# A bidirectional scan kernel: the forward direction's y is summed in PSUM instead of added afterwards

## The chip, the cores and the metric

The kernel runs on one core of a Trainium2 chip. The metric is the device time of one launch in microseconds (us). A core has TensorE (PE in the profile, its weight loads PEld), VectorE (DVE), ScalarE (ACT), GpSimd (POOL) and SyncE (SP, which issues the DMAs here). PSUM is the memory that TensorE writes into; DVE and ACT take results out of it.

## The reference, cut to what matters

The program is one convolution-attention hybrid: a selective state-space block with four scan directions, then attention without softmax, then a quantized feed-forward layer. The part that fills most of the time is the scan, for 8 images of 64 x 64 positions (L = 4096), 192 inner channels d, 16 states n and K = 4 directions:

```python
def step(h, inps):
    d_t, u_t, b_t, c_t = inps
    h = h * jnp.exp(d_t[..., None] * A) + (d_t * u_t)[..., None] * b_t[:, :, None, :]
    y = jnp.einsum('bkdn,bkn->bkd', h, c_t)
    return (h, y)
...
x_hwwh = jnp.stack([x_hw, x_wh], axis=1)
xs = jnp.concatenate([x_hwwh, jnp.flip(x_hwwh, axis=-1)], axis=1)
...
inv_y = jnp.flip(out_y[:, 2:4], axis=-1)
...
y = out_y[:, 0] + inv_y[:, 0] + wh_y + invwh_y
```

Directions 0 and 1 run forward over two orders of the positions (by rows, by columns); directions 2 and 3 run over the same two orders backwards. So y of direction 0 and of direction 2 are added position by position, and those of 1 and 3.

## The kernel before, in words

Every compute instruction is issued through a small class, `InOrder`, at one line, L91: so all rows of the profile name L91, and are told apart by their tiles. The order on each engine is fixed in advance: units of work are Python generators that `yield` an engine, a planned cost in us, a planned delay and sometimes a buffer to take, and a planner, `weave`, lets the unit go next whose engine and buffer are free first by those planned costs (rank decides ties). Each engine then runs its list strictly in that order on the chip. A changed cost or engine in one unit thus can change the order of the others.

The program has three passes. `pass1` makes the projections and the convolution, `pass2` the scans, `pass3` the rest. The change is in `pass2`. It works through 192 pieces, in order: 4 pairs of images, 3 chunks c of channels (chunks 0 and 1: the first 128 channels of one image each; chunk 2: the last 64 channels of both), 4 directions k, and 4 pieces of T = 1024 positions. For k of 2 and 3 the four pieces come in falling order of positions. An index `at` counts the pieces.

For each piece and each state n (16 of them):

- ACT makes `da` = exp(delta times A), 128 x 1024 (`decay`).
- The scan's other input is put into a `wide` tile in PSUM (two banks; there are three such tiles) in one of three ways, chosen by n: ACT scales the transposed `duT` to `x` and TensorE transposes it back into `wide` (8 transposes); POOL does the scaling (`xg`); or TensorE spreads b over the partitions (`wide<-xb,sel`) and DVE multiplies by `du` in place (`wide<-du,wide`). In chunks 0 and 1 these are 8, 2 and 6 of the 16 states, in chunk 2 they are 6, 3 and 7.
- DVE scans: `h<-da,carry,wide`. The scan ends the use of that `wide` tile. ACT keeps the last value for the next piece (`carry`).
- POOL multiplies two states at once by C, which a DMA has spread (`times_c`, the rows `c<-c,h`).
- TensorE adds these terms over n in `acc`, another PSUM tile of two banks, of which there is one: 8 transposes for each state, accumulated (`sum_over_n`, the rows `acc<-ident,c`). In pieces with k = 0 a term D times u (`ud`, made by ACT) comes first, as 8 more such transposes.

At the end of a piece `take_acc` empties `acc` into the tile `ys[k % 2]` (`y` in the profile) in SBUF: for k below 2 ACT copies it there; for k of 2 and 3 DVE adds it to what the piece of direction k - 2 at the same positions has left there. Then `acc` is free for the next piece's first sum, which waits for it. After the last piece of k = 2 and of k = 3, `store_y` writes the tile to memory, from where `pass3` reads it.

Of the kernel before, what the change touches and what calls it, by code (L numbers as in the profile page):

```python
# [42 lines left out]
P = 128  # L43
NB, HH, WW, C = 8, 64, 64, 96
L = HH * WW
DI, N, R, K = 192, 16, 6, 4
# [6 lines left out]
NT = T // P  # L53
# [5 lines left out]
GRP = 512  # L59
# [8 lines left out]
def chunk_rows(pair, c):  # L68

    b0 = 2 * pair  # L70
    if c < 2:
        return [(slice(0, P), b0 + c, slice(0, P))]
    return [(slice(64 * j, 64 * j + 64), b0 + j, slice(P, DI)) for j in range(2)]
# [456 lines left out]
def pass2(ctx, tc, g, ident, engines, fixed, u_d, xd_d, b_d, dt_d, y_d):  # L530
# [3 lines left out]
    pe, dve, act, pool = engines  # L534
# [4 lines left out]
    slots = {name: Slots(count) for name, count in room.items()}  # L539
# [4 lines left out]
    pieces = [  # L544
        (pair, c, k, NPC - 1 - i if k >= 2 else i) for pair in range(NB // 2) for c in range(3) for k in range(K) for i in range(NPC)
    ]
    done, counts, made, ys, carry = {}, {}, {}, {}, {}

    def take(name, shape, dtype=F32):

        return pools[name].tile(shape, dtype, name=name), slots[name].taken
# [203 lines left out]

    def sum_over_n(at, m):

        _, c, k, _ = pieces[at]

        def add(term, first, last):  # L760
            for i in range(NT):
                pe.matmul(
                    made["acc"][0][:, i, :], term[:, i * P : (i + 1) * P], ident, is_transpose=True,
                    start=first and i % (GRP // P) == 0, stop=last, skip_group_check=True,
                )

        if m == 0 and k == 0:
            yield "delta", at
            yield "act", 1.05, 0.2, slots["ud"]
            ud, slot = take("ud", [P, T])  # L770
            act.mul(ud, made[at][1], dsum[:, c // 2 : c // 2 + 1])
            end = yield "pe", 1.2, 0.0, slots["acc"]
            made["acc"] = take("acc", [P, NT, P])
            add(ud, True, False)
            slots["ud"].release(slot, end)
        yield "term", at, m
        for i in range(2):
            if m == 0 and k > 0 and i == 0:
                end = yield "pe", 1.2, 0.0, slots["acc"]
                made["acc"] = take("acc", [P, NT, P])  # L780
            else:
                end = yield "pe", 1.2, 0.0
            add(made["c", at, m][0][:, i, :], m == 0 and i == 0 and k > 0, 2 * m + i == N - 1)
        slots["c"].release(made["c", at, m][1], end)
        if m == N // 2 - 1:
            done["sum", at] = end

    def take_acc(at):
        pair, c, k, pc = pieces[at]
        o = k % 2  # L790
        yield "sum", at
        end = yield ("act", 0.95, 0.1) if k < 2 else ("dve", 1.2, 0.1)
        if at % (K * NPC) == 0:
            for i in range(2):
                ys[i] = one.tile([P, NBLK, P], F32, name=f"y{i}")
        acc, slot = made["acc"]
        dst = ys[o][:, pc * NT : (pc + 1) * NT, :]
        if k < 2:
            act.copy(dst, acc)
        else:  # L800
            dve.tensor_add(dst, dst, acc)
        slots["acc"].release(slot, end)
        if k >= 2 and at % NPC == NPC - 1:
            yield "sp", 2.0, 6.0
            store_y(ys[o], o, chunk_rows(pair, c))

    def store_y(y, o, parts):
        for part, b, ch in parts:
            if o == 0:
                sp.dma_start(y_d[b][0].rearrange("(i p) d -> p i d", p=P)[:, :, ch], y[:, :, part])  # L810
            else:

                rows = y_d[b][1].rearrange("(h i w) d -> w h i d", w=2, h=HH)
                for w in range(2):
                    sp.dma_start(rows[w][:, :, ch], y[w * HH : (w + 1) * HH, :, part])

    units = []
    for at, (pair, c, k, pc) in enumerate(pieces):
        by_act, by_pool = WAYS[c // 2]

        def add(kind, lead, unit, n=0):
            units.append((kind, at * N + n - lead, unit))

        add("prep", 8, prepare(at))
        for n in range(N):
            if n % 2 == 0:
                add("c", 12, load_c(at, n // 2), n)
            add("da", 2, decay(at, n), n)
            if n in by_act:
                add("x", 5, scaled(at, n), n)  # L830
            elif n in by_pool:
                add("xg", 4, scaled_by_pool(at, n), n)
            add("dbu", 1, products(at, n), n)
            add("scan", 0, scan(at, n), n)
            if n % 2 == 1:
                if at % NPC < NPC - 1:
                    add("carry", -2, carries(at, n // 2), n)
                add("term", 0, times_c(at, n // 2), n)
                add("sum", -4, sum_over_n(at, n // 2), n)
        add("acc", 0, take_acc(at), N)  # L840
# [289 lines left out]
```

## Time and profile before

| what | value |
|---|---|
| time, median of 3 runs | 10495.77 us (10492.87 to 10504.43) |
| time of the profiled execution | 10488.78 us |
| its span, first to last instruction | 10487.0 us |
| busy: TensorE matmuls, DVE, ACT, POOL | 7609.8, 9588.2, 9337.4, 9214.1 us |
| DVE adds `y<-y,acc` | 96, 1198 ns each |
| ACT copies `y<-acc` | 96, 990 ns each |
| first and last take-out of `acc` | starting at 827.87 and 9593.02 us |
| granted TensorE clock, mean | 0.898 |

The profile is of one execution. A row of a group has the engine, the operation, what is written and read with the shapes, the count, then busy us and mean ns, then the idle time of the engine just before these instructions and what ended it. For TensorE's rows the first name after the arrow is what streams through and the second is what is held in the array. A stretch of time has for each engine its busy us and, in brackets, the number of instructions.

### The profile page before, as it was taken

The numbers are of one execution on the slowest core, as the hardware profiler recorded it, in microseconds if no ns is written. First come the engines' busy times: TensorE is split into PE (matmuls) and PEld (weight loads), VectorE is DVE, ScalarE is ACT, GpSimd is POOL, SyncE is SP. The second block draws the span as 40 slices with busy tenths as digits, with TensorE's granted clock in tenths as the row PEclk, the third lists the DMA queues.
The fourth block names the chain that finished last, engine by engine and source line by source line (L and its number), as shares of the span: only waits on it lengthen the run. The fifth ranks groups of instructions, "written<-read, shape, count | busy, mean of one in ns | idle before, by whom it ended". The sixth has DMA issues, their size and how long they took to land.

```text
span 10487.0 us, 151319 instructions
## 1 busy us (share of the span) xinstructions
PE 7609.8 (73%) x51232; PEld 6209.7 (59%) x51232; DVE 9588.2 (91%) x6918; ACT 9337.4 (89%) x21427; POOL 9214.1 (88%) x3271
## 2 busy tenths in 40 slices
PE   6857777777677777776777777776777777776887
PEld 3326666656556666665566666665565666655766
DVE  6869999999999999999999999999999999997776
ACT  5759999999999999999999999999999999996665
POOL 1539999999999999999999999999999999997886
PEclk8878999998899999989999999889999999987776
DMA  5766776689976666789866666899766667997442
GB/s 149 237 184 213 218 232 212 213 210 200 202 216 210 215 217 207 217 200 200 216 210 213 216 212 214 203 201 203 218 209 216 218 203 219 201 199 179 127 132 59
DMA packets 928008, 2103.21 MB, mean 201 GB/s; under 512 B 274391, under 2 KB 422648, under 8 KB 925700
## 3 DMA queue, kind: packets, MB, share of 16 engines
q1 hardware_dynamic: 919812, 2092.79, 71.3%
q8 instruction: 410, 6.72, 0.3%
q14 instruction: 362, 2.97, 0.1%
q10 hardware_dynamic: 7424, 0.74, 0.1%
HBM read 1917.59 MB, written 175.66 MB: 200 GB/s over the span
## 4 chain that ended last, share of the span: by engine, by line
ACT 28%; DVE 21%; issue 18%; PE 16%; POOL 12%; DMA 4%; SPq 1%; ACTq 0%; DVEq 0%; POOLq 0%
DVE h L91 15%; ACT x L91 13%; ACT da L91 10%; POOL c L91 9%; PE acc L91 6%; PE wide L91 6%; DVE wide L91 3%; PE mm L91 2%; ACT L91 1%; POOL xg L91 1%; DMA xd_d<-xd 1%; DVE u L91 1%; DMA c<-xd_d 1%; PE px L91 1%; ACT delta L91 1%
## 5 line engine op out<-in xcount | busy, mean ns | idle before, releaser
L91 POOL TENSOR_TENSOR c<-c,h 128x2048 f32<-128x2048 f32 x1536 | 6965.9, 4549 | 378.0 <-DVE h L91 317.1
L91 DVE TENSOR_TENSOR_SCAN h<-da,carry,wide 128x1024 f32<-128x1024 f32 x2304 | 5253.5, 2330 | 214.7 <-PE wide L91 151.5
L91 ACT ACTIVATE x<-duT,bT 128x128 f32<-128x128 f32 (+1 forms) x14336 | 4158.4, 366 | 54.4 <-PE wide L91 48.2
L91 PE MATMUL acc<-ident,c 128*128 128x128 f32 x24576 | 3494.2, 298 | 540.5 <-POOL c L91 532.7
L91 ACT ACTIVATE da<-delta,a_neg 128x1024 f32<-128x1024 f32 x3072 | 3503.7, 1144 | 343.2 <-DVE h L91 332.3
L91 PEld LDWEIGHTS acc<-ident,c 128*128 128x128 f32 x24576 | 3145.3, 155 | 874.8 <-POOL c L91 737.0
L91 PE MATMUL wide<-ident,x 128*128 128x128 f32 x11264 | 1613.6, 291 | 857.7 <-DVE h L91 840.7
L91 PEld LDWEIGHTS wide<-ident,x 128*128 128x128 f32 x11264 | 1344.2, 149 | 1154.6 <-DVE h L91 511.3
L91 DVE TENSOR_TENSOR_SCAN h<-da,wide 128x1024 f32<-128x1024 f32 x768 | 1706.9, 2269 | 100.8 <-PE wide L91 69.7
L91 DVE TENSOR_TENSOR wide<-du,wide 128x1024 f32<-128x1024 f32 x1216 | 1458.4, 1211 | 130.8 <-PE wide L91 130.7
L91 PE MATMUL wide<-xb,sel 96*128 96x512 bf16 x2432 | 753.6, 394 | 582.4 <-DVE h L91 496.9
L91 POOL TENSOR_TENSOR xg<-duT,bT 128x512 f32<-128x512 f32 (+1 forms) x640 | 891.6, 1408 | 71.6 <-PE wide L91 51.1
L91 PEld LDWEIGHTS <-sel 96*128 96x128 bf16 x2432 | 224.2, 101 | 771.6 <-DVE h L91 374.1
L91 PE MATMUL wide<-ident,xg 128*128 128x128 f32 x3584 | 500.9, 285 | 239.8 <-DVE h L91 234.3
L91 PEld LDWEIGHTS wide<-ident,xg 128*128 128x128 f32 x3584 | 412.5, 146 | 316.8 <-issue 143.7
L91 POOL TENSOR_TENSOR du<-delta,u 128x1024 f32<-128x1024 f32 x192 | 455.1, 2370 | 154.4 <-ACT delta L91 145.1
L91 ACT ACT_TABLE_LOAD x385 | 494.0, 1283 | 6.8
L91 DVE SCALAR_TENSOR_TENSOR u<-xpad,conv_w,u 128x4096 f32<-128x4096 f32 x96 | 458.2, 4773 | 1.9
L91 PE MATMUL px<-u,w_xp 128*128 128x512 f32 x512 | 255.4, 638 | 80.8 <-ACT u L91 43.7
L91 PE MATMUL mm<-w_out,gt 128*128 128x96 f32 (+1 forms) x1024 | 262.7, 376 | 36.0 <-POOL gt L91 17.5
L91 POOL TENSOR_TENSOR bs<-bq,bs 128x512 bf16<-128x512 f32 (+1 forms) x48 | 123.9, 2583 | 155.9 <-ACT bs L91 144.6
L91 PEld LDWEIGHTS mm<-w_out,gt 128*128 128x128 f32 (+1 forms) x1024 | 201.2, 242 | 100.4 <-issue 32.8
(132 smaller groups left out, 5921.4 us busy)
## 6 DMA issues: line engine op xcount, KB each, us to landing
c<-xd_d SPq DMA_DIRECT2D x1024, 1024.0 KB
c<-xd_d SPq DMA_DIRECT2D x1024, 512.0 KB
u<-u_d SPq DMA_DIRECT2D x128, 512.0 KB
xdt<-dt_d SPq DMA_DIRECT2D x1152, 36.0 KB
xb<-b_d SPq DMA_DIRECT2D x384, 96.0 KB
u<-u_d SPq DMA_DIRECT2D x128, 256.0 KB
y_d<-y SPq DMA_DIRECT2D x24, 1024.0 KB
y<-y_d SPq DMA_DIRECT2D x64, 384.0 KB
```

The lines of the kernel that those rows point to most:

```text
L91: ins = getattr(self.engine, op)(*args, **kwargs).ins
```

## The change

For pieces with k of 2 or 3, the tile of the forward direction is now put into `acc` first, by 8 products of TensorE with the identity as the held operand (plain fp32 products, not transposes). The sums over n are then accumulated on top. The take-out is an ACT copy for every k; DVE's add is gone. The products take the `acc` buffer, so they stand in TensorE's list from the point where the planner sees `acc` free, with a planned cost of 1.5 us.

```diff
     def sum_over_n(at, m):
 
-        _, c, k, _ = pieces[at]
+        _, c, k, pc = pieces[at]
...
+        if m == 0 and k >= 2:
+
+            end = yield "pe", 1.5, 0.0, slots["acc"]
+            made["acc"] = take("acc", [P, NT, P])
+            for i in range(NT):
+                pe.matmul(
+                    made["acc"][0][:, i, :], ident, ys[k % 2][:, pc * NT + i, :],
+                    start=i % (GRP // P) == 0, stop=False, skip_group_check=True,
+                )
         yield "term", at, m
         for i in range(2):
-            if m == 0 and k > 0 and i == 0:
+            if m == 0 and k == 1 and i == 0:
                 end = yield "pe", 1.2, 0.0, slots["acc"]
                 made["acc"] = take("acc", [P, NT, P])
             else:
                 end = yield "pe", 1.2, 0.0
-            add(made["c", at, m][0][:, i, :], m == 0 and i == 0 and k > 0, 2 * m + i == N - 1)
+            add(made["c", at, m][0][:, i, :], m == 0 and i == 0 and k == 1, 2 * m + i == N - 1)
...
     def take_acc(at):
...
-        end = yield ("act", 0.95, 0.1) if k < 2 else ("dve", 1.2, 0.1)
+        end = yield "act", 0.95, 0.1
...
-        if k < 2:
-            act.copy(dst, acc)
-        else:
-            dve.tensor_add(dst, dst, acc)
+        act.copy(dst, acc)
```

## The prediction, made before the changed kernel was run

> **What bounds the kernel now.** I read the page first for the engines' shares, then cut the scan phase (827.9 to 9593.0 us, from the first to the last take-out of `acc`) into stretches of eight pieces, and read the busy time of each stretch. Then I read which waits are left on the fullest engine, and what the change's operations cost in the rows by shape.
>
> ```profile
> PE 7609.8 (73%) x51232; PEld 6209.7 (59%) x51232; DVE 9588.2 (91%) x6918; ACT 9337.4 (89%) x21427; POOL 9214.1 (88%) x3271
> ```
>
> Three engines share the load almost equally, so the mean names no bound. The stretches do. In order: pair 1, chunk 0, forward pieces (k 0 and 1); the same chunk reversed (k 2 and 3); then chunk 2 forward and reversed.
>
> ```profile
> core 0: us, PE busy (x) PEld busy (x) DVE busy (x) ACT busy (x) POOL busy (x), PEclk, DMA share, GB/s
> 2995.00:3352.00 357.00, 259.00 (x1936) 217.55 (x1936) 344.10 (x178) 342.55 (x743) 339.06 (x89) 0.95 0.68 214
> 3352.00:3717.00 365.00, 267.57 (x1912) 224.21 (x1912) 350.49 (x185) 336.12 (x731) 339.48 (x89) 0.93 0.66 212
> 4435.00:4813.00 378.00, 270.85 (x1896) 229.24 (x1896) 355.97 (x186) 372.82 (x996) 357.39 (x122) 0.90 0.91 205
> 4813.00:5193.00 380.00, 264.43 (x1848) 222.32 (x1848) 357.15 (x190) 363.09 (x963) 353.30 (x118) 0.91 0.91 204
> ```
>
> The reversed stretch of chunk 0 takes 8 us more than the forward one, and its DVE carries 6 us more while its ACT carries 6 less: DVE (96%) sets that stretch. In chunk 2 the forward stretch is ACT's (98.6%); the reversed one is nobody's alone (DVE 94%, ACT 96%, DMA 91%). What DVE waits for in the reversed stretch of chunk 0 (3352 to 3717), from the waits of that window (us in total, times, longest), is TensorE's filling of `wide`:
>
> ```profile
> DVE h L91 <- PE wide L91: 12.3, 8, 2.1
> ```
>
> 12.3 us of the 14.5 that DVE is idle there. So what matters for a piece is DVE's work, and TensorE coming in time with the next `wide`.
>
> The time per piece, from the starts of the 192 take-outs in the timeline (the first five left out), by k:
>
> - chunks 0 and 1: k0 44.70, k1 44.50, k2 45.91, k3 45.54 us; k2 and k3 together 45.72 (64 pieces).
> - chunk 2: k0 47.93, k1 46.77, k2 47.27, k3 47.43; k2 and k3 together 47.35 (32 pieces).
>
> **What the Trainium skill says.** "FP8 and Floating Point Precision", TensorE Precision Notes: a true fp32 product takes four passes through the array. "Perfetto Trace Analysis", Transposes: a transpose has special logic that skips the arithmetic. The trace agrees that a plain fp32 product is dearer: `px` has 256 calls and 512 records, two for each call, where a transpose has one. "TensorE: Matmul & The Clock Gate", Step-by-step: what each phase is for: matmuls stay in program order, only weight loads are pulled ahead. So a matmul that waits holds up the fillings of `wide` behind it.
>
> **The change part by part.**
>
> ```profile
> L91 DVE TENSOR_TENSOR y<-y,acc 128x1024 f32<-128x1024 f32 x96 | 115.0, 1198 | 16.2 <-PE acc L91 16.2
> L91 ACT COPY y<-acc 128x1024 f32<-128x1024 f32 x96 | 95.0, 990 | 0.6 <-PE acc L91 0.6
> ```
>
> 1. Removed: 96 adds on DVE, one for each reversed piece, 1.198 us each: 115 us of DVE's queue, and 16 us in which DVE stood before them for TensorE's last sum.
> 2. Added: 96 copies on ACT at 0.990 us, 95 us. The forward pieces do exactly this already. Behind a waiting copy on ACT stand `da` and `x`, which feed the scans; the 0.6 us of idle time before 96 such copies says that the planner puts them where `acc` is ready.
> 3. Added on TensorE: 8 plain fp32 products of 128 columns for each reversed piece, 768 in all, the built order confirms; no other instruction changes in number, and no DMA does. The trace has none of this shape. Nearest:
>
> ```profile
> 9814.15 1.03 PE L91 MATMUL mm<-weff,lnT 97*128 97x96 f32 x8
> ...
> 699.80 8.32 PE L91 MATMUL px<-u,w_xp 128*128 128x512 f32 x19
> ```
>
> A record of 96 columns comes each 0.13 us (1.03 / 8), one of 512 each 0.438 (8.32 / 19): 0.00074 us a column. For 128 columns that is 0.13 + 32 x 0.00074 = 0.154, so 16 records are 2.5 us a piece, or 236 us of TensorE. At the half clock, where the `w_out` row shows 0.333 us a record (16 in 5.33), they would be up to 5.3 us; with the weight load wholly hidden, 1.6 (0.00074 x 128 x 16). I take 2.5. In the reversed stretch TensorE then goes from 268 to 288 us of some 357, 81%: it is not full.
> 4. A new wait: the first `acc<-y` of a piece needs ACT's copy of the piece before. In the built order it stands one filling of `wide` behind the last sum of that piece, directly ahead of another filling or of the first sums. Before, the first `acc<-c` had the same kind of wait (for DVE's add), but mostly behind POOL's term, which came later anyway.
>
> What the pieces take without the add can be read from k1: it has the same scans, products, `da`, `x` and one ACT copy, and neither the `ud` of k0 nor the add. If a reversed piece becomes like k1, chunks 0 and 1 gain 45.72 - 44.50 = 1.22 us x 64 = 78 us, chunk 2 gains 47.35 - 46.77 = 0.58 x 32 = 19 us: **97 us**. As a check, DVE falls from 350.5 to 340.9 and ACT rises from 336.1 to 344.0 in the reversed stretch, nearly the forward stretch's pair (344.1 and 342.6), which took 357.
>
> What k1 lacks is TensorE's 2.5 us. It is hidden as long as DVE has filled `wide` buffers: three exist, so with one just filled, two more are ahead, some 2 x 2.25 us of scans (289.9 / 129 in that stretch) and now and then a product of 1.21. At a handover around 3393 us I followed it: the last sum ends at 3393.4, a filling is done at 3394.2, ACT's next free place is near 3394.6 or 3395.9, so the copy is done near 3396; 2.5 us of products and 1.1 us for the filling behind them end near 3399.5, and DVE, without its add, wants that filling at about 3399.2. So it is at the edge: I take 0.4 us for each reversed piece, between 0 (k0's eight extra transposes, waiting for ACT's `ud` in the same place, leave k0 only 0.2 us over k1 in chunks 0 and 1) and 1.0 (the overshoot above where both the copy and the clock are late). 96 x 0.4 = 38 us.
>
> Sum: -97 + 38 = **-59 us**. Against the profiled execution, 10488.8 us (span 10487.0 and 1.8 around it), that is 10429.8. The median of the runs shown, 10495.8, stands 7.0 above that execution, so the forecast is **10437 us**, 0.6% under. The last take-out, at the end of the phase, changes by 0.2 us and counts nothing; the passes before and after keep their instructions.
>
> **The rivals.** A measurement of this kernel can tell about 0.2% (21 us) from no change.
>
> - *ACT takes over in chunk 2.* There ACT is at 96% in reversed stretches and gets 8 x 0.99 = 7.9 us more in 380, so 98%. If all of that adds to the time, chunk 2 loses 32 x 0.99 = 32 us, in place of gaining 19: -78 + 32 + 38 = -8 us, 10488. For it: the forward stretch, where k0's `ud` of 1.14 us shows as 1.16 us a piece. Against: k1 carries the copy and is the fastest kind there.
> - *DVE was not the bound* (the pieces are held by POOL, 93%, or by DMA in chunk 2): nothing moves, 10496. Against: POOL does the same in forward stretches in 8 us less.
> - *TensorE's block starves DVE: slower.* The place is the first `acc<-y`: TensorE stands there for ACT's copy, up to 2.1 us (a `da` of 1.14 under way and 0.99), then works 2.5, and every filling of `wide` behind it is late. Against a stock of 4.5 us of scans, with 1.1 for the filling itself, DVE loses up to 1.2 us at full clock; with a part of the products at the half clock some 2.0. It decides from 1.0 us a piece on (97 / 96). At 2.0: -97 + 192 = +95, 10591. For it: TensorE's fillings are the one thing DVE waits for now. Against: the forward pieces wait little for that copy, as the row of who `acc` waited for says:
>
> ```profile
>   ACT y L91: 26.2, 24
> ```
>
> 26 us over 96 copies, both TensorE rows counted.
>
> **How the numbers follow.** Main case 0.74; ACT takes over in chunk 2 0.07; no bound moved 0.06; starved 0.13. Main lies over 0.2% faster but for 0.02, the first rival in a third of its cases, the second never, and starved ends slower but for 0.01: faster 0.75, within 0.2% 0.12, slower 0.13. The range: low end, all 97 us and 14 more if the pieces pack tighter than k1 does (their DVE and ACT work, 341 and 344 us, still leaves 13 of 357): 10385. High end: starvation of 1.0 us cancels the gain, 10496, and a little over it: 10505. Beyond it lies most of the starved case, some 0.12; below it 0.06.
>
> **What would show it.** In the profile after: DVE in reversed stretches of chunk 0 near 341 us and ACT near 344, stretches of about 358 to 360 us in place of 365; those of chunk 2 at 376 to 380; `acc<-y` in 1536 records spaced about 0.15 us; DVE's waits for `wide` up by less than 40 us in all. Wrong would be: those waits up by over 100 us, or long waits of TensorE for ACT's `y`, with reversed pieces at 46 us or more; or chunk 2 alone longer, with ACT at 98%.

## The result, and the profile after

The changed kernel took 10450.2 us (median of 5 runs, 10442.2 to 10451.8), before 10495.8 on the same chip: ratio 0.9953, 95% interval 0.9939 to 0.9968, a gain of some 46 us. Forecast were 10437 and a gain of 59. The profiled execution has a span of 10446.9 us, 40.1 less than before. 8.2 of these lie ahead of the first take-out of `acc` (819.6 against 827.9 us), where the order on the engines is unchanged. The other runs of this study have this first take-out anywhere from 809.5 to 824.5, so that part is scatter between executions; 31 us come from the scan phase.

The engines' shares on the page after:

```profile
PE 7673.1 (73%) x52768; PEld 6378.4 (61%) x52768; DVE 9496.8 (91%) x6822; ACT 9405.8 (90%) x21523; POOL 9212.9 (88%) x3271
```

The 96 adds have left DVE, 96 copies are on ACT, and TensorE has 1536 records more. DVE's busy time fell by 91 us, not by 115: its other instructions show 24 us more. The same four stretches of eight pieces as before (pair 1: chunk 0 forward, chunk 0 reversed, chunk 2 forward, chunk 2 reversed):

```profile
core 0: us, PE busy (x) PEld busy (x) DVE busy (x) ACT busy (x) POOL busy (x), PEclk, DMA share, GB/s
2968.00:3327.00 359.00, 261.39 (x1938) 226.92 (x1939) 343.09 (x178) 343.10 (x743) 337.42 (x89) 0.92 0.67 213
3327.00:3689.00 362.00, 267.46 (x2034) 235.47 (x2033) 342.16 (x177) 340.61 (x736) 338.65 (x89) 0.93 0.65 213
4410.00:4790.00 380.00, 271.79 (x1880) 231.98 (x1880) 354.40 (x186) 372.74 (x996) 356.68 (x122) 0.88 0.92 204
4790.00:5166.00 376.00, 277.99 (x1992) 239.20 (x1992) 351.05 (x183) 368.31 (x971) 354.47 (x118) 0.90 0.91 206
```

The reversed stretches fell from 365 to 362 and from 380 to 376 us. In chunk 0 DVE and ACT are even now (342 and 341), yet the stretch still needs 20 us more than either. The take-out and the products, in the groups by shape:

```profile
L91 ACT COPY y<-acc 128x1024 f32<-128x1024 f32 x192 | 190.2, 991 | 16.4 <-PE acc L91 16.3
L91 PE MATMUL acc<-y,ident 128*128 128x128 f32 x1536 | 206.4, 291 | 57.0 <-ACT y L91 56.9
```

What DVE waits for, from the waits of the whole run (total us, times, longest):

```profile
DVE h L91 <- PE wide L91: 276.9, 159, 5.3
DVE wide L91 <- PE wide L91: 115.0, 98, 21.7
```

The same two before:

```profile
DVE h L91 <- PE wide L91: 221.3, 149, 5.0
DVE wide L91 <- PE wide L91: 130.7, 115, 22.4
```

Together they rose by 39.9 us, which is almost what the forecast took off (38 us). TensorE's idle time for ACT's `y`, at the products, is 57 us: 35 of the 96 blocks of products waited, 31 of them up to 2.0 us and four between 4.3 and 5.0. The four are at the first reversed piece of chunk 2 in each pair, and there DVE ran dry. One of them, from the timeline (start, length, engine, instruction, count, idle time before it and what ended it):

```profile
4785.44 0.60 PE L91 MATMUL wide<-xb,sel 96*128 96x512 bf16 x2
...
4789.24 1.00 ACT L91 COPY y<-acc 128x1024 f32<-128x1024 f32 x1
...
4790.29 3.78 PE L91 MATMUL acc<-y,ident 128*128 128x128 f32 x16 [4.26 <-ACT y L91]
...
4793.87 1.54 PE L91 MATMUL wide<-ident,x 128*128 128x128 f32 x8
...
4795.52 4.46 DVE L91 TENSOR_TENSOR_SCAN h<-da,wide 128x1024 f32<-128x1024 f32 x2 [4.31 <-PE wide L91]
```

TensorE stands for ACT's copy, works the products, and only then makes the filling for which DVE stands 4.31 us. The four stalls are 17.8 us of DVE's idle time together.

From the trace, two things are worked out for each run: the time per piece by k (from the starts of the take-outs), and DVE's idle time per piece, by the scan before which it lies.

| | chunks 0, 1: k0, k1, k2, k3 (us a piece) | chunk 2: k0, k1, k2, k3 |
|---|---|---|
| before | 44.70, 44.50, 45.91, 45.54 | 47.93, 46.77, 47.27, 47.43 |
| after | 43.96, 45.52, 45.13, 45.40 | 48.08, 46.87, 47.32, 46.41 |

The forward piece k1, to whose instructions nothing was done, became 1.02 us slower, and k0 0.74 faster. In chunks 0 and 1 most of DVE's idle time is at one place, before the tenth scan (state 9). There it was 1.31 us a piece in k1 and 1.70 in reversed pieces (mean of k2 and k3); after the change 1.76 and 2.09. At that place TensorE makes `delta`'s product for the next piece into one of the three `wide` tiles. ACT holds that tile through a table load and the activation (1.28 and 1.11 us in the piece shown), and TensorE makes the filling for state 9 (POOL's `xg`) after it. From the timeline after, the rows of TensorE and then the scan of DVE:

```profile
3381.64 1.87 PE L91 MATMUL acc<-ident,c 128*128 128x128 f32 x8 [2.30 <-POOL c L91]
3383.31 1.06 PE L91 MATMUL wide<-xdt,dt_w 108*128 108x512 bf16 x2
3384.16 1.54 PE L91 MATMUL acc<-ident,c 128*128 128x128 f32 x8
3385.54 1.04 PE L91 MATMUL wide<-ident,xg 128*128 128x128 f32 x8
...
3386.69 4.58 DVE L91 TENSOR_TENSOR_SCAN h<-da,carry,wide 128x1024 f32<-128x1024 f32 x2 [2.44 <-PE wide L91]
```

Here TensorE stands 2.30 us for POOL's term, so `delta`'s product and the filling `wide<-ident,xg` come late, and DVE stands 2.44 us. This is far from the start of the piece, where the new products are.

### The profile page after: what moved, and what is told of

Its sections match the earlier page's. It is cut to its first block, busy times and chain, and to the rows that moved or that the text cites. A ratio compares the mean times of both kernels' runs of the same rounds, so it can differ in the third digit from the quotient of the medians.

```text
span 10446.9 us, 154273 instructions
## 1 busy us (share of the span) xinstructions
PE 7673.1 (73%) x52768; PEld 6378.4 (61%) x52768; DVE 9496.8 (91%) x6822; ACT 9405.8 (90%) x21523; POOL 9212.9 (88%) x3271
## 4 chain that ended last, share of the span: by engine, by line
ACT 43%; DVE 17%; PE 15%; issue 14%; POOL 7%; DMA 4%; SPq 1%; ACTq 0%; DVEq 0%; POOLq 0%
ACT x L91 19%; ACT da L91 16%; DVE h L91 12%; PE acc L91 6%; PE wide L91 4%; POOL c L91 3%; DVE wide L91 3%; ACT L91 2%; PE mm L91 2%; ACT y L91 1%; ACT delta L91 1%; DMA xd_d<-xd 1%; ACT duT L91 1%; PE px L91 1%; PE pa L91 1%
## 5 line engine op out<-in xcount | busy, mean ns | idle before, releaser
L91 PE MATMUL acc<-ident,c 128*128 128x128 f32 x24576 | 3451.6, 296 | 653.8 <-POOL c L91 648.8
L91 PE MATMUL wide<-ident,x 128*128 128x128 f32 x11264 | 1573.2, 287 | 661.1 <-DVE h L91 634.6
L91 PEld LDWEIGHTS wide<-ident,xg 128*128 128x128 f32 x3584 | 448.0, 153 | 175.3 <-issue 84.3
L91 PE MATMUL wide<-ident,du 128*128 128x128 f32 x1536 | 213.8, 284 | 106.3 <-DVE h L91 77.9
L91 PEld LDWEIGHTS wide<-ident,du 128*128 128x128 f32 x1536 | 176.3, 146 | 137.7 <-issue 86.4
```

Source lines behind the costliest of these rows:

```text
L91: ins = getattr(self.engine, op)(*args, **kwargs).ins
```

## The experiments

Ratios are to the kernel before on the same chip, with 95% intervals; each median is of 5 to 13 runs.

| kernel | median us | ratio |
|---|---|---|
| changed kernel | 10450.2 | 0.9953 (0.9939 to 0.9968) |
| e1: no products, same order | 10454.3 | 0.9962 (0.9948 to 0.9976) |
| e3: two products of 512 columns, same order | 10459.9 | 0.9967 (0.9955 to 0.9980) |
| e2: DVE copies | 10490.9 | 0.9997 (0.9989 to 1.0005) |
| e4: products later | 10419.8 | 0.9930 (0.9917 to 0.9942) |
| e5: later, 512 columns | 10416.5 | 0.9934 (0.9921 to 0.9946) |
| e8: no products, no step | 10418.9 | 0.9936 (0.9923 to 0.9948) |
| e9: products in the first sum's step | 10420.2 | 0.9934 (0.9921 to 0.9946) |
| e10: planned cost 0.1 | 10418.6 | 0.9931 (0.9919 to 0.9944) |
| e12: products before the seventh pair | 10419.1 | 0.9931 (0.9918 to 0.9945) |
| e7: planned cost 2.0 | 10525.6 | 1.0030 (1.0019 to 1.0042) |
| e6: before, add planned at 1.0 | 10508.2 | 1.0022 (1.0013 to 1.0031) |
| e11: before, add planned at 1.4 | 10484.7 | 0.9992 (0.9984 to 1.0000) |

**e1, the products left out, the order kept.**

```diff
             made["acc"] = take("acc", [P, NT, P])
-            for i in range(NT):
-                pe.matmul(
-                    made["acc"][0][:, i, :], ident, ys[k % 2][:, pc * NT + i, :],
...
-            add(..., m == 0 and i == 0 and k == 1, 2 * m + i == N - 1)
+            add(..., m == 0 and i == 0 and k > 0, 2 * m + i == N - 1)
```

> The changed kernel without the products of the identity with y: the forward direction's y is left out of the sum, so this part of the computation is missing. The order of all other instructions on every engine is the changed kernel's. Theory 1 (TensorE's block of products, 1.95 us, and its wait for ACT's copy keep the change from its full gain): about 38 us below the changed kernel, so near 10412 us, with DVE's waits for wide back near the 350 us of before. Theory 2 (the products cost nothing; the gain fell short since the new plan orders the pieces worse): within 10 us of the changed kernel, 10440 to 10460.

Measured: 0.9962, nothing gained. DVE's waits for `wide` are 272.3 and 119.3 us, in total as much as with the products, though not at the same places: none of the four stalls of over 4 us is in this trace, and the first reversed piece of chunk 2 takes 47.2 us in place of 49.1 (means of four). That is 8 us in all, less than these runs can tell (the interval is 15 us either way). So the rise of 40 us in the waits, which fits the forecast's sum so well, comes without the products too. The first theory fell: neither TensorE's 1.95 us a piece nor the wait in front of them is a loss of some 38 us.

**e3, fewer and wider products, the order kept.**

```diff
-            for i in range(NT):
-                pe.matmul(
-                    made["acc"][0][:, i, :], ident, ys[k % 2][:, pc * NT + i, :],
-                    start=i % (GRP // P) == 0, stop=False, skip_group_check=True,
+            for q in range(0, NT, GRP // P):
+                pe.matmul(
+                    made["acc"][0][:, q : q + GRP // P, :], ident, ys[k % 2][:, pc * NT + q : pc * NT + q + GRP // P, :],
+                    start=True, stop=False, skip_group_check=True,
```

> The changed kernel with two products of 512 columns in place of eight of 128 for each reversed piece, the order otherwise the same. From the px row (0.438 us a record, four records) 1.75 us a piece in place of the 1.95 measured. Theory 1: the block's length counts, but only 0.2 us of it goes: 0 to 10 us below the changed kernel, 10440 to 10450. Theory 2: no change.

Measured: 0.9967, no faster. The block hardly got shorter (1.88 us for the four records against 1.95; each of these is the commonest length, in about half of the pieces), so this run alone says little; it does not contradict e1.

**e2, the take-out back on DVE, as a copy.**

```diff
-        end = yield "act", 0.95, 0.1
+        end = yield ("act", 0.95, 0.1) if k < 2 else ("dve", 1.2, 0.1)
...
-        act.copy(dst, acc)
+        (act.copy if k < 2 else dve.tensor_copy)(dst, acc)
```

> The changed kernel, but in reversed pieces DVE copies acc out in place of ACT. DVE then has a copy of about 1.2 us where it had the add, ACT has nothing added, TensorE has the products. Theory 1 (what was gained is DVE's 1.2 us a piece, what was lost is TensorE's block): nothing is gained and the block is still paid, 10496 plus up to 38 us: 10500 to 10535. Theory 2 (products free): 10490 to 10500, but for what the plan moves. If the kernel stays near 10450, DVE's load was not what the change relieved.

Measured: 0.9997, as before. The group of the copies:

```profile
L91 DVE COPY y<-acc 128x1024 f32<-128x1024 f32 x96 | 115.4, 1202 | 13.5 <-PE acc L91 13.4
```

A copy out of PSUM costs DVE what the add cost, 1.20 us. So the change's gain is that the take-out leaves DVE, and the 768 products show no cost here either, as far as one plan can tell.

**e4, the products before the fifth pair of states.**

```diff
-        if m == 0 and k >= 2:
-            end = yield "pe", 1.5, 0.0, slots["acc"]
-            made["acc"] = take("acc", [P, NT, P])
+        if m == 4 and k >= 2:
+            yield "pe", 1.5, 0.0
...
-                    start=i % (GRP // P) == 0, stop=False, skip_group_check=True,
+                    start=False, stop=False, skip_group_check=True,
```

> The changed kernel with the products moved from the start of the piece to just before the fifth pair of states (m = 4), where acc is in use anyway: no wait for ACT's copy is left in front of them, and the first sum starts acc as it did before the change. Theory 1: TensorE's waits for ACT's y (57 us at the products) go, the block stays: 10 to 25 us below the changed kernel, 10425 to 10440. Theory 2 (plan): up or down by up to 20 us with no relation to those waits.

Measured: 0.9930, 30 us below the changed kernel, a little past what the first theory gave. With e1 that theory can't explain it; e4 also has another order on every engine. The next four kernels part the work from the order.

**e8, the take-out alone.** Products and their step are gone from `sum_over_n`; the first sum starts `acc` for every k above 0; ACT copies.

> The changed kernel without the products and without their step in the plan: reversed pieces start acc with the first sum, ACT copies it out, and the forward direction's y is missing from the result. This is the take-out moved from DVE to ACT and nothing else, with a plan of its own. Theory A (the products' work is free; their planned step at the start of the piece gives a worse order): as fast as the kernel with the products later, 10410 to 10425, 30 us below the changed kernel. Theory B (the moved take-out alone gives the order with the longer stall at the tenth state): near the changed kernel, 10440 to 10460. Theory C (the estimate of the prediction, reversed pieces like those of k1): 97 us below before, about 10395.

**e9, the products within the first sum's step.**

```diff
                 end = yield "pe", 1.2, 0.0, slots["acc"]
                 made["acc"] = take("acc", [P, NT, P])
+                if k >= 2:
+                    for j in range(NT):
+                        pe.matmul(
+                            made["acc"][0][:, j, :], ident, ys[k % 2][:, pc * NT + j, :],
+                            start=j % (GRP // P) == 0, stop=False, skip_group_check=True,
+                        )
```

> The changed kernel with the products issued within the step of the first sum, after its wait for POOL's first term, with no step and no cost of their own in the plan: the order of everything else is that of the kernel without products and step. Theory A (products' work is free wherever TensorE is not waited for): within 10 us of that kernel. Theory B (1.95 us of TensorE in front of the first sum delays fillings of wide): 15 to 40 us above it.

**e5, e4 with two products of 512 columns.** The edits of e4 and e3 together.

> Products later (before the fifth pair of states) and as two of 512 columns in place of eight of 128; the order is that of the kernel with the products later. Theory A (the products' work is free): within 10 us of that kernel's 10420. Theory B (TensorE's time counts): 10 us or more below it, under 10410.

Measured: e8 0.9936, e9 0.9934, e5 0.9934. Theory A holds: with the same order, with and without the products, the time is the same within the intervals of some 13 us (e8 against e9), wide or narrow products give the same (e4 against e5), and the changed kernel's 10450 is not the price of the products. The estimate of the prediction, 97 us for the take-out alone, is not reached: e8 gains 67 us (0.0064 of 10487). Its pieces show why. In chunks 0 and 1 the reversed ones take 44.96 us and k1 takes 45.02: they did become like k1, but k1 itself went up from 44.50. The reversed pieces gain 76 us together (0.76 x 64 in chunks 0 and 1, 0.87 x 32 in chunk 2), and the forward ones lose about 9 in sum.

**e6 and e11, controls: the kernel before with only a planned cost changed.**

```diff
-        end = yield ("act", 0.95, 0.1) if k < 2 else ("dve", 1.2, 0.1)
+        end = yield ("act", 0.95, 0.1) if k < 2 else ("dve", 1.0, 0.1)
```

e11 has 1.4 in this place.

> The kernel before with nothing changed but the planned cost of DVE's add, 1.0 in place of 1.2: the same instructions in another order, a control for what a new plan does by itself. If new plans move the time by little: within 10 us of before. If the order matters as much as the change: 15 us or more off, either way, and differences of that size between kernels with different plans are not to be put down to the instructions.

> The kernel before with the planned cost of DVE's add at 1.4 in place of 1.2: the second control of what a new plan does without a change of instructions. At 1.0 the time went up by 0.22%. If plans scatter around before: anything from 10465 to 10520. If before's plan is near the best for its instructions: at or above 10487 again.

Measured: 1.0022 and 0.9992. The same instructions in another order move by 0.2% one way and by about 0.1% the other (the interval just reaches 1); the order alone can be worth half of what the change brought.

**e10 and e7, the changed kernel with only the planned cost of the products' step changed,** to 0.1 and to 2.0:

```diff
-            end = yield "pe", 1.5, 0.0, slots["acc"]
+            end = yield "pe", 0.1, 0.0, slots["acc"]
```

> The changed kernel with one number changed: the planned cost of the products' step, 0.1 in place of 1.5. The step still takes acc at the start of the piece; the order on ACT and DVE becomes that of the kernel with the products in the first sum, and TensorE's order differs from that one only in where the products stand. If the planned cost made the worse order: 10410 to 10430, as that kernel. If the early place before the first sum, with its wait for ACT's copy, was the loss: near the changed kernel's 10450.

> The changed kernel with the planned cost of the products' step at 2.0, about what the trace shows (1.95 us), in place of 1.5. If the plan is better where its costs are truer: faster than the changed kernel by 10 us or more. If the cost only shifts the order by chance, or if any cost at this place pushes fillings back: within 15 us of 10450, or slower.

Measured: 0.9931 and 1.0030. One number in the plan, with all instructions the same, takes the kernel from 0.7% faster to 0.3% slower; and the number nearest to the truth is the worst. e10 keeps the early place before the first sum and, but for the products, has the order of e9 on all engines; it equals e9, so that place with its wait costs nothing here that the runs could tell. Its trace has eight handovers where DVE stands 3.6 to 4.5 us behind the products (the first pieces of k2 and of k3 in chunk 2), and e9's has none; what they cost comes back within the following pieces: the reversed pieces of chunk 2 take 46.53 us in e10 and 46.47 in e9. Between the changed kernel and e10 the scan phase, from the first to the last take-out, differs by 42 us (8733.8 against 8692.2). DVE's idle time in the four kinds of piece of chunks 0 and 1 together is 8.60 against 7.63 us; over all these pieces that is 31 of the 42 us, 20 of them before the tenth scan. In chunk 2 it is 12.53 against 12.26, 4 us.

e7 shows at full size the starved case that the prediction had as its slower rival. Its chunk 2, reversed (pair 1), as a stretch (columns as above):

```profile
4804.00:5198.00 394.00, 280.89 (x1992) 244.39 (x1992) 349.55 (x183) 366.81 (x966) 353.62 (x118) 0.89 0.86 194
```

and the same of e10:

```profile
4774.00:5146.00 372.00, 271.51 (x1991) 232.01 (x1991) 347.91 (x183) 363.95 (x964) 351.45 (x118) 0.93 0.91 207
```

22 us more for eight pieces, with hardly a change in DVE's and ACT's work. One handover of e7, from the timeline of all engines:

```profile
4846.24 1.91 PE L91 MATMUL acc<-ident,c 128*128 128x128 f32 x16
...
4848.09 2.00 ACT L91 ACTIVATE x<-duT,bT 128x64 f32<-128x64 f32 x8
...
4850.00 1.13 ACT L91 ACTIVATE da<-delta,a_neg 128x1024 f32<-128x1024 f32 x1
...
4851.04 0.17 ACT L91 COPY carry<-h 128x2 f32<-128x2 f32 x1
4851.12 1.06 ACT L91 ACTIVATE x<-duT,bT 128x64 f32<-128x64 f32 x4
...
4852.09 1.13 ACT L91 ACTIVATE da<-delta,a_neg 128x1024 f32<-128x1024 f32 x1
...
4853.12 0.99 ACT L91 COPY y<-acc 128x1024 f32<-128x1024 f32 x1
...
4854.16 3.78 PE L91 MATMUL acc<-y,ident 128*128 128x128 f32 x16 [6.01 <-ACT y L91]
...
4857.74 1.92 PE L91 MATMUL wide<-ident,x 128*128 128x128 f32 x8
...
4859.76 2.35 DVE L91 TENSOR_TENSOR_SCAN h<-da,carry,wide 128x1024 f32<-128x1024 f32 x1 [5.59 <-PE wide L91]
```

The last sums end at 4848.15. Here the plan put no filling of `wide` between them and `acc<-y`. ACT has five groups of work in front of its copy and gets to it at 4853.12; TensorE stands 6.0 us, then works the products at a granted clock of 0.50 (in the stretch 4854 to 4857.8), 3.78 us in place of 1.95, and only then comes the filling; DVE has used up its stock and stands 5.59 us. Waits of 3.6 to 6.0 us with such a stall of DVE behind them come in 24 of the 32 reversed pieces of chunk 2; in the other eight TensorE waits 0.8 to 1.5 us and DVE hardly stands. The reversed pieces of chunk 2 take 49.21 us, 2.7 more than in e10: 86 of the 117 us between the two spans (10527.5 and 10410.7). Why e10's eight stalls cost next to nothing and these so much is not shown. One reason why ACT is behind there is in the code: a step of `scaled` is planned at 0.6 us, and in chunk 2 its four instructions take 1.05 (ACT rows above), in chunks 0 and 1 its two take some 0.65 (1.26 for four). That this error makes ACT late was not tried by a run.

**e12, the products before the seventh pair:** e4 with `m == 6`.

> The products before the seventh pair of states in place of the fifth. If any place with no wait in front is as good: 10410 to 10430. If the plan's order decides: up to 30 us more, though the instructions are the same.

Measured: 0.9931. Six kernels with the take-out on ACT (e4, e5, e8, e9, e10, e12), in three different plans, lie within 4 us of each other, 10416.5 to 10420.2. That they lie so close is in part chance: e12's reversed pieces take 44.55 us in chunks 0 and 1, the shortest of all, and 47.38 in chunk 2, as long as before (47.35); there DVE stands 2.3 us a piece before the tenth scan. All six beat both the kernel before and the changed one. Three in the changed kernel's plan (itself, e1, e3) lie at 10450 to 10460. The version to keep is any of the five that have the products; e10 is the change with one number altered.

## Why the prediction was right, point by point

- **The bound and the sign: right.** DVE's add set the reversed stretches of chunks 0 and 1. Taking it off DVE gave the gain (e8), giving a copy back to DVE took all of it away (e2, 0.9997). These kernels differ in their plans as well, but none of the four plans with the take-out on DVE (before, e2, e6, e11) has a median under 10484, and of the five with it on ACT four lie from 10417 to 10460; the fifth is e7's. ACT had room, in chunk 2 too: it is at 98% there (368 of 376 us), and yet the rival in which ACT takes over didn't come, the reversed pieces of chunk 2 fell from 47.35 to 46.87 us.
- **Step "reversed pieces become like k1": right in kind, its term too large.** 97 us were forecast, e8 measured 67. The prediction took k1's time from the old plan as if it were fixed. Under e8's plan reversed pieces do equal k1 (44.96 and 45.02), but k1 has 45.02 in place of 44.50.
- **Step 3, the products' work: too large, and without an effect that shows.** 2.5 us a piece were estimated from two other shapes; the block takes 1.95 or 2.05 in 86 of the 96 pieces and 3.3 to 3.8 in ten. (The lower bound beside it, 0.00074 x 128 x 16, is 1.5 and not 1.6; nothing hung on it.) Where 0.4 us a piece (38 us) was taken off, the metric shows no price beyond the intervals of some 13 to 15 us: e1, and e8 against e9.
- **Step 4, the wait for ACT's copy: there, mostly covered, and at four handovers longer than was thought.** 35 of the 96 blocks waited, 31 of them in chunk 2. The short waits left DVE's stock intact but for one (1.06 us). In the four long ones ACT had a `da`, a `carry` and two groups of `x` in front of its copy, not the one `da` of the prediction, and DVE stood 4.3 to 4.5 us. Even so chunk 2's reversed pieces became faster on the whole.
- **What the forecast didn't have: the plan.** The products' step at 1.5 us in the plan costs the changed kernel 18 to 23 us by the ratios (0.9953 against 0.9931 and 0.9936; the intervals overlap by 0.0005 and 0.0009) and about 31 by the medians; the six kernels above against the three show the same step. It stands in the place of the 38 us that were forecast for starvation. So the sum came out near by luck, two errors that met: a gain taken 30 us too large, and a loss that is some 20 us in place of 38 and mostly has another reason; -67 + 21 is the measured -46. The sign that "DVE's waits for `wide` rise by less than 40 us" was met just so, 39.9, and still meant something else, since e1 has the rise without the products.
- **The slower rival: its mechanism is real.** The place, TensorE standing at `acc<-y` with the fillings behind it, and the half clock are as described; it is there four times in the changed kernel, and e7 ends 0.3% slower, for the most part by it. The products are the same in all these kernels; what differs is how much stands between the last sums and them in the order, and how late ACT is by then.

What stays open: which exchange in the order makes the tenth scan's wait longer at a planned cost of 1.5 than at 0.1. The orders differ in hundreds of places on TensorE and ACT; no single one was tried.

## What to carry to other kernels

Where a planner orders the work by estimated costs, an edit moves the order as well as the work, so a control with the same instructions and another plan belongs beside every result under one per cent: here the spread of plans was 0.3% for the kernel before and 1.0% for the changed one. A forecast from "this piece will look like that one" needs the same allowance, for that one is planned anew too. And a wait added at the head of an in-order engine can become dear when its releaser is late, as e7's handovers show: keep other work of that engine in front of it (argued, not tried by itself), or put the waiting work where its input has long been ready, as e4 and e12 do. No block of products waits for ACT's copy there, and in e4 all 96 take 1.95 us.

## What the runs showed of the hardware that was not expected

- Plain fp32 products of 128 columns with the same held operand start one record each 0.112 us at full clock, and 16 take 1.95 us. That is quicker than the 0.154 interpolated in the prediction. `weff`'s records of 96 columns, with other weights for each, mostly start each 0.112 us too: the 0.13 read there was the length of a block of eight over its count, and so spread the longer last record (0.275 us) over few.
- Two products of 512 columns take 1.88 us, eight of 128 take 1.95: hardly any cost for the loads of weights between the narrow ones.
- A wait of 6.0 us in front of TensorE was followed by a block at a granted clock of 0.50, so one late release cost TensorE 6.0 us and 1.8 more. "TensorE: Matmul & The Clock Gate" of the Trainium skill, What's actually happening, states that the clock falls to half after an idle window of some 3.4 us. In the changed kernel the four waits of 4.3 to 5.0 us, each followed by a block of 3.78, agree. Of the 31 waits up to 2.0 us, 26 were followed by blocks of 2.05, but five, of 1.3 to 1.85 us, by blocks of 3.27 or 3.28 at a granted clock of 0.59. Here the clock also fell after single idle times far shorter than 3.4 us, so what a wait costs in clock can't be told from its length alone.
